# A two-layer graph network: counting edges with one matmul a group, weighing a node's own row by its number of self-edges, and spreading one step of the sort over five groups

## The chip, the core and the metric

The kernel runs on one core of a Trainium2 chip. The metric is the time of one whole execution on the device, in microseconds (us); before the change it is 2135.78 us, the median of three runs from 2135.06 to 2137.22. The five engines named below run their own instruction streams in the order in which the program gave them: TensorE (PE) for matmuls and transposes, VectorE (DVE), ScalarE (ACT), GpSimd (POOL), which here issues the indirect DMAs, and SyncE (SP), which here issues the plain ones.

## The reference

There are 6250 nodes of 512 float32 values and 106,250 directed edges: 50,000 random ones, the same ones reversed, and one self-edge for each node, all sorted by destination. Among the random ones a few are self-edges too, so a node can have more than one. Two layers follow each other:

```python
# layer 0 (edges sorted by dst)
agg = segment_sum((x @ W_l.T + b_l)[src], dst);  deg = segment_sum(1, dst)
x   = layernorm(x + agg / max(deg, 1) + x @ W_r.T)
# layer 1 (sums over src: the edges have to be sorted by src)
neigh = segment_sum((x[dst] @ W_neigh.T + b_neigh), src) / max(segment_sum(1, src), 1)
h   = x + relu(x @ W_self.T + b_self + neigh)
h   = layernorm(h) * gamma + beta
x   = layernorm(x + h)
```

The text calls them first and second layer. Both take a mean over a node's edges of rows gathered from a table (the input x, then the first layer's result h), and multiply mean and own row by one 512x512 matrix each.

## The kernel before

**Tiles, windows, groups.** The sorted edges lie 128 to a tile, one edge on each partition. POOL gathers the 128 rows of a tile with one indirect DMA from the table (`gather`, L603, issued at L604): 128 rows of 2 KB. The nodes are cut into windows of at most 32 consecutive ones, and four windows (C = 4) far apart in the list make a group, which fills 128 partitions. The first layer has 831 tiles, 238 windows and 60 groups; the second 782 tiles, 261 windows and 66 groups, since the sort of the second layer drops each node's first self-edge, whose row is the node's own and needs no gathering. The groups at the end have three windows. A buffer named `rows` holds one tile for each of the four windows, and there are ten such buffers (CHUNKS), so gathers can run ahead of their use by up to ten of them.

**One group.** `fetch` (L608) issues the group's gathers, about 14 in the first layer and 12 in the second (nine in the last three groups). `match` (L628) makes the 0/1 matrix `hot` on DVE: for every tile and window, which of the window's 32 nodes the edge on each partition belongs to. `visits` (L685) sums the rows: one matmul per tile and window, `hot` (128x32) against the gathered rows (128x512), into `agg` in PSUM (L694). `shrink` (L636) makes a bfloat16 copy `hotb` of `hot` on ACT (L639). `count` (L697) multiplies `hotb`, tile by tile, by a column of ones, which gives the number of edges of each node in `deg` (L703): 600 such matmuls in all, four or five a group. `inverse` (L553) makes one over it on DVE (L557 in the second layer, L560 to L563 in the first). `average` (L708) multiplies `agg` by it on ACT (L714). `turn` transposes on PE (L569), `dense` multiplies by the two weight matrices (L577), `close` and `store` (L732) do the rest of the layer on DVE and write the group's rows through SP (L743), or, for three groups of each layer, through POOL with an indirect scatter (L736). `begin` (L669) loads the group's own rows through SP (L682).

**Self-edges in the second layer.** The first self-edge of each node is added as the node's own row: `average` adds `own` to `agg` on DVE before the mean (L712, shown under the line of the helper `both`, L173), and `inverse` adds 1 to the count (L557). Self-edges beyond the first, of which up to 64 are allowed (CAP), are put into one extra tile of rows, `more_rows`, gathered once at the head of the second layer (L611, by the list `more_i`). Every group of the second layer visits it like a tile of its own (X = 1), at the head of `visit_tiles`: 522 matmuls in all, eight instructions a group with their weight loads.

**What packs that list.** The second layer's sort runs inside the first layer's groups. `sort_and_place` (L891) yields it as small pieces, and `more` takes one PE piece and up to five DVE pieces out of the list at the end of each group. The last two PE pieces are `loops_beyond_one` (L386) and `place` (L441). `loops_beyond_one` finds the self-edges beyond the first among the last 51 columns of sorted edges, numbers them, builds one 0/1 matrix for each column on DVE (in chunks of 14 columns, in one buffer `hots`), and multiplies it with the column on PE (L430) into 64 slots; 102 matmul instructions. It is one piece. `place` then finds where the windows begin.

**The order of the work.** There is no planner: on each engine the instructions stand in the program's order. The loop at the end of `grouped` writes that order out by hand. In one turn of it, gathers and `hot` of group g+1 come first, then visits of group g in three parts, with the transposes and matrix products of group g-1 between them, then count and average of g, the finish of g-1, a piece of the sort, and `hotb` of g+1.

Of the kernel before, what the change touches and what calls it, by code (L numbers as in the profile page):

```python
# [19 lines left out]
C = 4  # L20
# [78 lines left out]
def kernel(  # L99
# [109 lines left out]
    class Sorter:  # L209


        def __init__(self, key, val, layer, pool, ps, loops):


            self.pool, self.ps, self.layer, self.loops = pool, ps, layer, loops
            self.M = M if not loops else (E - N + P - 1) // P
            pair = self.pair = PAIR_L if loops else PAIR
            self.half = (pair + 1) // 2
            self.vis = self.half + 1
            self.NW = (2 * self.M + pair - 1) // pair  # L220
# [12 lines left out]
            self.flag = const.tile([1, 1], I32, name=f"flag{layer}")  # L233
            if loops:

                a = (E - N - CAP - 1) // P
                self.row = pool.tile([P, M - a], F32, name="row")
                nc.gpsimd.iota(self.row, pattern=[[P, M - a]], base=a * P - (E - N) + LOOP,
                               channel_multiplier=1, allow_small_or_imprecise_dtypes=True)
                self.more = const.tile([P, 1], F32, name="more")  # L240
                self.more_i = const.tile([P, 1], I32, name="more_i")
# [144 lines left out]
        def loops_beyond_one(self):  # L386
# [35 lines left out]
            per = W // CAP  # L422
            hots = self.fresh()
            for m in range(0, n, per):
                k = min(per, n - m)
                hot = hots[:, :k * CAP].rearrange("p (k c) -> p k c", c=CAP)
                both(hot, number[:, m:m + k].unsqueeze(2).to_broadcast([P, k, CAP]),
                     iota[:, :CAP].unsqueeze(1).to_broadcast([P, k, CAP]), ALU.is_equal)
                for i in range(k):
                    nc.tensor.matmul(p[:CAP, D + 2:D + 3], hot[:, i, :], node[:, m + i:m + i + 1],  # L430
                                     start=m + i == 0, stop=m + i == n - 1)
# [6 lines left out]
            nc.vector.tensor_scalar(none, self.more, float(N - 1), None, op0=ALU.min)  # L438
            nc.vector.tensor_copy(self.more_i, none)
# [113 lines left out]
    def inverse(deg, nr, work, loops=False):  # L553

        inv = work.tile([P, 1], F32, name="inv")
        if loops:
            nc.vector.tensor_scalar(inv[:nr], deg, 1.0, None, op0=ALU.add)  # L557
            nc.vector.reciprocal(inv[:nr], inv[:nr])
            return inv, None
# [20 lines left out]
    def grouped(s, table, w_n, w_s, layer, finish, dest, other):  # L580


        with tc.tile_pool(name=f"g{layer}", bufs=2) as work, tc.tile_pool(
# [24 lines left out]
            def fetch(g):  # L608
                if g == 0 and s.loops:
                    rows = work.tile([P, D], F32, name="more_rows", bufs=1)  # L610
                    nc.gpsimd.indirect_dma_start(  # L611
                        out=rows, out_offset=None, in_=table,
                        in_offset=bass.IndirectOffsetOnAxis(ap=s.more_i[:, :1], axis=0))
                    chunks["more"] = {c: rows for c in range(C)}
# [21 lines left out]
            def shrink(g):  # L636
                hb = work.tile([P, (s.X + s.vis) * C, H], BF16, name="hotb", bufs=1)
                n = len(visit_tiles(g)) * C
                nc.scalar.copy(hb[:, :n], hots[g][:, :n])  # L639
# [45 lines left out]
            def visits(g, some):  # L685
# [4 lines left out]
                for v, t in list(enumerate(visit_tiles(g)))[some]:  # L690
                    for c in windows(g):
                        ts = [u for u in visit_tiles(g) if c in chunks[u]]
                        if t in ts:
                            nc.tensor.matmul(agg[H * c:H * (c + 1), :], hot[:, C * v + c, :],  # L694
                                             chunks[t][c], start=t == ts[0], stop=t == ts[-1])

            def count(g):  # L697
                st, hb = state[g], hots[g][1]
                nr = st["nr"]
                deg = ps.tile([P, 1], F32, name="deg")  # L700
                n = len(visit_tiles(g))
                for v in range(n):
                    nc.tensor.matmul(deg[:nr],  # L703
                                     hb[:, C * v:C * v + nr // H, :].rearrange("p c h -> p (c h)"),
                                     ones_b, start=(v == 0), stop=(v == n - 1))
# [55 lines left out]
            for g in range(Q + 1):  # L761
# [5 lines left out]
                if g < Q:  # L767
                    visits(g, slice(0, 2 + s.X))
# [172 lines left out]
```

## Time and profile before

| | |
|---|---|
| time, three runs | 2135.78 us (2135.06 to 2137.22) |
| the profiled execution's own time | 2607.48 us |
| its span, first to last instruction | 2605.5 us |
| mean granted TensorE clock | 0.904 of full speed |
| PE busy | 1986.7 us, 76%, 8653 matmul instructions |
| POOL busy | 1554.8 us, 60% |
| DVE busy | 1045.7 us, 40% |
| ACT busy | 368.7 us, 14% |
| visits, L694 (gathered tiles; `more_rows`) | 4220 instructions, 780.1 us; 522, 71.4 us |
| count, L703 | 600 instructions, 35.8 us, 167 ns each |
| `hotb`, L639 | 126 casts, 86.3 us, 685 ns each |
| `agg` plus `own`, L173 | 66, 46.2 us, 700 ns each |
| packing's matmuls, L430 | 102 instructions, 11.4 us |
| `more_rows` gather, L611 | 1, 1.0 us |

Durations and waits come from one profiled execution, which here took 2607.48 us where the timed runs took 2135.78. A profile line names the source line, the engine, the operation, what it writes and reads, how often it ran, its busy time and the mean of one in ns, and the idle time of the engine just before it with what ended it. "Issue" stands for idle time for which the profile shows no cause. A row of a timeline has the start in us from the span's first instruction, the duration, then engine, line and operation; a bracket at its end holds the engine's idle time ahead of it and what ended that. Several equal instructions that follow each other are one row (x4).

### The profile page before, as it was taken

Reading aid. Unit: us, or ns where it says so; the run is one execution under the profiler, and the core shown is the slowest. Engines: PE = TensorE matmul, PEld = TensorE weight load, DVE = VectorE, ACT = ScalarE, POOL = GpSimd, SP = SyncE. Lnnn points to the kernel's source line nnn. Section 1 sums busy time; section 2 is a strip of 40 time slices with the busy share of each in tenths; the row PEclk is TensorE's granted clock in tenths of the full one; section 3 lists DMA queues with packets and bytes.
Section 4 is the critical chain, followed back from the end, with each engine's and each line's share of the span. In section 5 each row is a group of like instructions: output and inputs, shape, how many; then the busy total and the mean of one; then the engine's idle time right before and its main releaser. Section 6 shows DMA issues by size and latency. Waiting matters only on the chain.

```text
span 2605.5 us, 27728 instructions
## 1 busy us (share of the span) xinstructions
PE 1986.7 (76%) x8653; PEld 725.9 (28%) x8653; DVE 1045.7 (40%) x2301; ACT 368.7 (14%) x721; POOL 1554.8 (60%) x1639
## 2 busy tenths in 40 slices
PE   4186876877778676776674888888888888888896
PEld 1022322322322223322220232332323223232332
DVE  2244333344444343211220454444544445454465
ACT  0011111111111111111110111111111111111121
POOL 4566666666666664566526666666656666666641
PEclk9698888888898887898886999999999999999999
DMA  7666766666676664666526676666666676666752
GB/s 222 182 196 203 211 198 204 207 202 202 201 209 202 204 201 147 179 205 205 164 79 183 201 203 202 204 206 204 198 200 204 201 210 199 202 194 204 206 170 59
DMA packets 184614, 499.74 MB, mean 192 GB/s; under 512 B 43962, under 2 KB 46452, under 8 KB 184446
## 3 DMA queue, kind: packets, MB, share of 16 engines
q0 software_dynamic: 130208, 426.37, 56.3%
q1 hardware_dynamic: 51406, 65.89, 8.0%
q10 hardware_dynamic: 2832, 5.51, 0.6%
q8 instruction: 74, 1.21, 0.2%
q14 instruction: 94, 0.77, 0.1%
HBM read 465.01 MB, written 32.96 MB: 191 GB/s over the span
## 4 chain that ended last, share of the span: by engine, by line
PE 37%; issue 14%; another core or an unknown queue 12%; DVE 9%; SPq 4%; ACT 1%; DMA 1%; POOL 0%; DVEq 0%; POOLq 0%; ACTq 0%
PE po L577 19%; PE agg L694 14%; PE tp L569 3%; SPq L743 2%; SPq L644 1%; SPq L682 1%; DVE stats L505 1%; DVE agg L173 1%; DVE po L173 1%; DVE srt L173 1%; ACT mean L714 1%; DVE hot L173 1%; DVE po L515 1%; DVE y L515 1%
## 5 line engine op out<-in xcount | busy, mean ns | idle before, releaser
L604 POOL DMA_INDIRECT rows<-in_x_dram,idx x834 | 799.9, 959 | 468.4 <-issue 238.8
L604 POOL DMA_INDIRECT rows<-h_d,idx x785 | 744.6, 948 | 437.1 <-issue 211.3
L694 PE MATMUL agg<-rows,hot 128*32 128x512 f32 x4220 | 780.1, 633 | 222.9 <-issue 186.0
L577 PE MATMUL po<-wa,meanT 128*128 128x512 f32 (+1 forms) x1008 | 492.2, 633 | 86.8 <-issue 81.3
L577 PE MATMUL po<-wb,ownT 128*128 128x512 f32 (+1 forms) x1008 | 488.6, 630 | 0.3
L694 PEld LDWEIGHTS agg<-rows,hot 128*32 128x32 f32 x4220 | 148.4, 111 | 657.9 <-issue 589.7
L560 DVE TENSOR_SCALAR inv<-deg 128x1 f32<-128x1 f32 (+1 forms) x60 | 9.5, 158 | 786.2 <-remote 312.5
L577 PEld LDWEIGHTS po<-wa,meanT 128*128 128x128 f32 (+1 forms) x1008 | 189.8, 198 | 391.1 <-issue 382.1
L569 PE MATMUL tp<-ident,mean 128*128 128x128 f32 (+1 forms) x504 | 97.5, 325 | 215.0 <-ACT mean L714 146.0
L557 DVE TENSOR_SCALAR inv<-deg 128x1 f32<-128x1 f32 (+1 forms) x66 | 10.5, 158 | 619.6 <-remote 401.4
L577 PEld LDWEIGHTS po<-wb,ownT 128*128 128x128 f32 (+1 forms) x1008 | 196.1, 206 | 207.3 <-issue 204.5
L571 ACT COPY ownT<-tp 128x512 f32<-128x512 f32 (+1 forms) x126 | 73.3, 582 | 1193.2 <-remote 495.9
L173 DVE SCALAR_TENSOR_TENSOR srt<-srt 128x448 f32<-128x448 f32 (+3 forms) x313 | 180.7, 618 | 4.6
L569 PEld LDWEIGHTS tp<-ident,mean 128*128 128x128 f32 (+1 forms) x504 | 63.1, 162 | 350.0 <-ACT mean L714 218.3
L714 ACT ACTIVATE mean<-agg,inv 128x512 f32<-128x512 f32 (+1 forms) x126 | 86.6, 687 | 391.1 <-DVE some L563 83.1
L509 ACT ACTIVATE rstd<-mv,eps 128x1 f32<-128x1 f32 (+1 forms) x192 | 56.6, 295 | 426.1 <-DVE mv L507 204.0
L571 ACT COPY meanT<-tp 128x512 f32<-128x512 f32 (+1 forms) x126 | 72.5, 575 | 183.6 <-remote 122.2
L173 DVE SCALAR_TENSOR_TENSOR hot<-rel,cols 128x640 f32<-128x640 f32 x126 | 96.2, 765 | 0.1
L639 ACT CAST hotb<-hot 128x640 bf16<-128x640 f32 x126 | 86.3, 685 | 24.5 <-DVE hot L173 24.5
L569 PEld LDWEIGHTS tp<-ident,own 128*128 128x128 f32 (+1 forms) x504 | 62.6, 141 | 67.5 <-issue 65.5
L694 PE MATMUL agg<-more_rows,hot 128*32 128x512 f32 x522 | 71.4, 611 | 13.1 <-DMA rows<-h_d,idx 13.1
L569 PE MATMUL tp<-ident,own 128*128 128x128 f32 (+1 forms) x504 | 75.2, 272 | 0.0
(154 smaller groups left out, 968.1 us busy)
## 6 DMA issues: line engine op xcount, KB each, us to landing
own<-h_d SPq DMA_DIRECT2D x261, 64.0 KB
out_dram<-y SPq DMA_DIRECT2D x250, 64.0 KB
own<-in_x_dram SPq DMA_DIRECT2D x230, 64.0 KB
h_d<-y SPq DMA_DIRECT2D x227, 64.0 KB
rows<-in_x_dram,idx POOLq DMA_INDIRECT x834
rows<-h_d,idx POOLq DMA_INDIRECT x785
wa<-in_L_gnn_W_l_dram ACTq DMA_DIRECT2D x1, 1024.0 KB
wb<-in_L_gnn_W_r_dram ACTq DMA_DIRECT2D x1, 1024.0 KB
```

The costliest lines, as they stand in the source:

```text
L173: nc.vector.scalar_tensor_tensor(o, a, 1.0, b, op0=ALU.mult, op1=op)
L505: nc.vector.bn_stats(stats[:nr], v)
L509: nc.scalar.activation(root[:nr], mv[:nr, 1:2], AF.Sqrt, bias=eps[:nr])
L515: nc.vector.tensor_scalar(y, v, mv[:nr, 0:1], root[:nr], op0=ALU.subtract, op1=ALU.mult)
L569: nc.tensor.transpose(p[:, k, :nr], v[:nr, k * P:(k + 1) * P], ident[:nr, :nr])
L571: nc.scalar.copy(t[:, :, :nr], p[:, :, :nr])
L577: nc.tensor.matmul(po[:nr], aT[:, k, :nr], w[:, k, :], start=first and k == 0, stop=end and k == NK - 1)
L604: nc.gpsimd.indirect_dma_start(out=t, out_offset=None, in_=table, in_offset=bass.IndirectOffsetOnAxis(ap=s.idx[:, m:m + 1], axis=0))
L639: nc.scalar.copy(hb[:, :n], hots[g][:, :n])
L694: nc.tensor.matmul(agg[H * c:H * (c + 1), :], hot[:, C * v + c, :], chunks[t][c], start=t == ts[0], stop=t == ts[-1])
L714: nc.scalar.mul(st["mean"][:nr], st["agg"][:nr], st["inv"][:nr])
L743: put.append(nc.sync.dma_start(dest[ds(start(c * Q + g, dest), H), :], y[H * c:H * (c + 1)]))
```

## The change

- **Count.** `shrink` no longer casts `hot`. It sums `hot` over the tiles of the group on DVE (`tensor_reduce`, with a stride, since the tiles are the outer index) and writes the sum, 128x128 in bfloat16, into `hotb`. `count` is then one matmul, into a column of `deg`. In the second layer ACT copies the part of `hot` that marks the extra self-edges into a second half of `hotb`, and a second matmul counts them by themselves.
- **Own row.** `average` in the second layer adds `own` times (1 + number of extra self-edges) to `agg`, in one instruction on DVE, instead of `own` once. The count's inverse takes one more small DVE operation.
- **No extra tile of rows.** `more_rows`, its gather, its list `more_i` and its visits are gone; the parts of the visits are cut at the same gathered tiles as before (0:2, 2:3, 3:).
- **Packing in pieces.** `loops_beyond_one` is now a generator with five pieces; each of the later ones has the matmuls of up to 14 columns, whose matrices were made in the piece before, in two halves of `hots` with seven columns each. It takes five groups, and `place` comes four groups later.

```diff
-                self.more_i = const.tile([P, 1], I32, name="more_i")
+                self.parts = 2 + (M - a - 1) // (W // CAP // 2 * 2)
...
-            per = W // CAP
+            per = W // CAP // 2
             hots = self.fresh()
-            for m in range(0, n, per):
+
+            def hot(m):
                 k = min(per, n - m)
-                hot = hots[:, :k * CAP].rearrange("p (k c) -> p k c", c=CAP)
-                both(hot, number[:, m:m + k].unsqueeze(2).to_broadcast([P, k, CAP]),
+                v = hots[:, m // per % 2 * per * CAP:][:, :k * CAP].rearrange(
+                    "p (k c) -> p k c", c=CAP)
+                both(v, number[:, m:m + k].unsqueeze(2).to_broadcast([P, k, CAP]),
                      iota[:, :CAP].unsqueeze(1).to_broadcast([P, k, CAP]), ALU.is_equal)
-                for i in range(k):
-                    nc.tensor.matmul(p[:CAP, D + 2:D + 3], hot[:, i, :], node[:, m + i:m + i + 1],
-                                     start=m + i == 0, stop=m + i == n - 1)
+                return v
+
+            ready = [(m, hot(m)) for m in range(0, min(2 * per, n), per)]
+            while ready:
+                yield
+                for m, v in ready:
+                    for i in range(v.shape[1]):
+                        nc.tensor.matmul(p[:CAP, D + 2:D + 3], v[:, i, :],
+                                         node[:, m + i:m + i + 1],
+                                         start=m + i == 0, stop=m + i == n - 1)
+                m += per
+                ready = [(m, hot(m)) for m in range(m, min(m + 2 * per, n), per)]
...
-    def inverse(deg, nr, work, loops=False):
+    def inverse(deg, nr, work):
         inv = work.tile([P, 1], F32, name="inv")
-        if loops:
-            nc.vector.tensor_scalar(inv[:nr], deg, 1.0, None, op0=ALU.add)
-            nc.vector.reciprocal(inv[:nr], inv[:nr])
-            return inv, None
...
             def fetch(g):
-                if g == 0 and s.loops:
-                    rows = work.tile([P, D], F32, name="more_rows", bufs=1)
-                    nc.gpsimd.indirect_dma_start(
-                        out=rows, out_offset=None, in_=table,
-                        in_offset=bass.IndirectOffsetOnAxis(ap=s.more_i[:, :1], axis=0))
-                    chunks["more"] = {c: rows for c in range(C)}
...
             def visit_tiles(g):
                 t = own_tiles(g)
-                return ["more"] * s.X + list(range(t.start - 1, t.stop))
+                return range(t.start - 1, t.stop)
...
             def shrink(g):
-                hb = work.tile([P, (s.X + s.vis) * C, H], BF16, name="hotb", bufs=1)
-                n = len(visit_tiles(g)) * C
-                nc.scalar.copy(hb[:, :n], hots[g][:, :n])
+                hb = work.tile([P, 1 + s.X, C * H], BF16, name="hotb", bufs=1)
+                n = s.X + len(visit_tiles(g))
+                with nc.allow_low_precision("whole numbers up to 5"):
+                    nc.vector.tensor_reduce(
+                        hb[:, 0, :], hots[g][:, s.X * C:n * C].rearrange(
+                            "p (v c) h -> p (c h) v", c=C),
+                        axis=mybir.AxisListType.X, op=ALU.add)
+                if s.X:
+                    nc.scalar.copy(hb[:, 1, :], hots[g][:, :C].rearrange("p c h -> p (c h)"))
                 hots[g] = (hots[g], hb)
...
             def count(g):
-                deg = ps.tile([P, 1], F32, name="deg")
-                n = len(visit_tiles(g))
-                for v in range(n):
-                    nc.tensor.matmul(deg[:nr],
-                                     hb[:, C * v:C * v + nr // H, :].rearrange("p c h -> p (c h)"),
-                                     ones_b, start=(v == 0), stop=(v == n - 1))
-                st["inv"], st["some"] = inverse(deg[:nr], nr, work, s.loops)
+                deg = ps.tile([P, 2], F32, name="deg")
+                for i in range(1 + s.X):
+                    nc.tensor.matmul(deg[:nr, i:i + 1], hb[:, i, :nr], ones_b,
+                                     start=True, stop=True)
+                if not s.loops:
+                    st["inv"], st["some"] = inverse(deg[:nr, :1], nr, work)
+                    return
+                st["some"] = None
+                for n in ("loops", "inv"):
+                    st[n] = work.tile([P, 1], F32, name=n)
+                nc.vector.tensor_scalar(st["loops"][:nr], deg[:nr, 1:2], 1.0, None, op0=ALU.add)
+                nc.vector.tensor_tensor(st["inv"][:nr], deg[:nr, :1], st["loops"][:nr],
+                                        op=ALU.add)
+                nc.vector.reciprocal(st["inv"][:nr], st["inv"][:nr])
...
                 if s.loops:
-                    both(st["agg"][:nr], st["agg"][:nr], st["own"][:nr], ALU.add)
+                    nc.vector.scalar_tensor_tensor(st["agg"][:nr], st["own"][:nr],
+                                                   st["loops"][:nr], st["agg"][:nr],
+                                                   op0=ALU.mult, op1=ALU.add)
...
-                    visits(g, slice(0, 2 + s.X))
+                    visits(g, slice(0, 2))
...
-                    visits(g, slice(2 + s.X, 3 + s.X))
+                    visits(g, slice(2, 3))
...
-                    visits(g, slice(3 + s.X, None))
+                    visits(g, slice(3, None))
...
-        yield True, s.loops_beyond_one
+        parts = s.loops_beyond_one()
+        for _ in range(s.parts):
+            yield True, lambda: next(parts, None)
         yield True, s.place
```

More of the change, by code (lines that the diff above doesn't have):

```diff
@@ L437, in loops_beyond_one @@
             nc.vector.tensor_scalar(self.more, self.more, float(-LOOP), None, op0=ALU.add)
-            nc.vector.tensor_scalar(none, self.more, float(N - 1), None, op0=ALU.min)
-            nc.vector.tensor_copy(self.more_i, none)
         def place(self):
@@ L625, in visit_tiles @@
                 t = own_tiles(g)
-                return ["more"] * s.X + list(range(t.start - 1, t.stop))
+                return range(t.start - 1, t.stop)
             def match(g):
                 hot = work.tile([P, (s.X + s.vis) * C, H], F32, name="hot")
-                n = len(visit_tiles(g)) * C
+                n = (s.X + len(visit_tiles(g))) * C
                 both(hot[:, :n], s.rel[:, g].rearrange("p v c -> p (v c)")[:, :n].unsqueeze(2)
@@ L636, in shrink @@
             def shrink(g):
-                hb = work.tile([P, (s.X + s.vis) * C, H], BF16, name="hotb", bufs=1)
-                n = len(visit_tiles(g)) * C
-                nc.scalar.copy(hb[:, :n], hots[g][:, :n])
+                hb = work.tile([P, 1 + s.X, C * H], BF16, name="hotb", bufs=1)
[7 more added lines that the diff above has]
+                    nc.scalar.copy(hb[:, 1, :], hots[g][:, :C].rearrange("p c h -> p (c h)"))
                 hots[g] = (hots[g], hb)
@@ L693, in visits @@
                         if t in ts:
-                            nc.tensor.matmul(agg[H * c:H * (c + 1), :], hot[:, C * v + c, :],
+                            nc.tensor.matmul(agg[H * c:H * (c + 1), :],
+                                             hot[:, C * (s.X + v) + c, :],
                                              chunks[t][c], start=t == ts[0], stop=t == ts[-1])
```

## The prediction

> **What bounds the kernel now.** I read the groups first, then the timelines of the layers' ends and middle, and put the result beside the times. The groups (columns: executions, busy us, mean ns of one, idle us before them):
>
> ```profile
> L604 POOL DMA_INDIRECT rows<-in_x_dram,idx x834 | 799.9, 959 | 468.4 <-issue 238.8
> L604 POOL DMA_INDIRECT rows<-h_d,idx x785 | 744.6, 948 | 437.1 <-issue 211.3
> ...
> L639 ACT CAST hotb<-hot 128x640 bf16<-128x640 f32 x126 | 86.3, 685 | 24.5 <-DVE hot L173 24.5
> ...
> L694 PE MATMUL agg<-more_rows,hot 128*32 128x512 f32 x522 | 71.4, 611 | 13.1 <-DMA rows<-h_d,idx 13.1
> ```
>
> PE is busiest by its share (76% against POOL's 60%), so one would take PE for the bound. The timeline of the second layer's start says otherwise:
>
> ```profile
> 1370.91 0.95 POOL L604 DMA_INDIRECT rows<-h_d,idx  x1 [0.30 <-issue]
> 1372.17 0.95 POOL L604 DMA_INDIRECT rows<-h_d,idx  x1 [0.30 <-issue]
> 1373.42 0.95 POOL L604 DMA_INDIRECT rows<-h_d,idx  x1 [0.30 <-issue]
> 1376.91 0.28 PE L703 MATMUL deg<-ones_b,hotb 128*128 128x1 bf16 x5
> ```
>
> A POOL that waits for nothing starts a gather every 1.25 us: 0.95 of work and a gap of 0.30 that follows every gather. Group 0's last gather starts at 1372.17 and its count at 1376.91: PE is 4.7 us behind, so transfers keep up. In the middle of the layer it looks different:
>
> ```profile
> 2219.23 1.03 PE L694 MATMUL agg<-rows,hot 128*32 128x512 f32 x4
> 2222.40 1.02 PE L694 MATMUL agg<-rows,hot 128*32 128x512 f32 x2 [2.14 <-issue]
> 2225.72 0.94 POOL L604 DMA_INDIRECT rows<-h_d,idx  x1 [4.28 <-PE agg L694]
> ```
>
> PE sits between its instructions with "issue" named, on rows gathered some 50 us before, and POOL waits for it. These waits are in the profiled execution (2607.48 us) and, I infer, hardly in the timed runs (2135.78 us). The proof is a sum of POOL's schedule with those waits left out, from rows alone:
> - first gather at 30.4;
> - layer 1: 834 x (0.959 + 0.305) = 1054.2, two other gathers and two iotas 3.0;
> - handover: 4.7 to the last group's count, 0.7 by which PE's last group (12.0) exceeds its nine gathers (11.3), 19.4 from that count (1333.9) to the next gather (1353.3): 24.8;
> - layer 2: the extra gather 1.3, 785 x (0.948 + 0.305) = 983.6, two scatters in the queue 2.6;
> - end: 4.7, PE's lag in the last three groups 2.2 (below), and 23.8 from the last count (2581.7) to 2605.5: 30.7.
>
> Sum 2130.6; with the 2.0 around the span 2132.6, against 2135.8 timed: 0.15% short. So in the timed runs **POOL's gather rate sets the time**, 12 gathers = 15.0 us a group in layer 2, about 14 = 17.6 in layer 1, while PE without those waits needs 14.2 (2523.34 to 2537.55) in layer 2 and 14.0 (991.93 to 1005.93) in layer 1.
>
> **The change, part by part.** Lines are those of before.
>
> *The extra gather* (L611): one POOL gather at the head of layer 2, 1.00 + 0.30: **-1.3 us**. The other gathers, the own loads and the stores keep number and order in the POOL and SP queues.
>
> *The extra visits* (L694, more_rows): 522 instructions, eight a group, pitch about 0.88 us a group, so 58 us of PE. In steady state this lies inside POOL's 15.0 us and is worth nothing. It counts where PE is behind POOL: the last three groups have three windows, nine gathers (11.3 us), and PE takes 12.9:
>
> ```profile
> 2537.55 0.28 PE L703 MATMUL deg<-ones_b,hotb 128*128 128x1 bf16 x5
> 2537.76 1.06 PE L694 MATMUL agg<-more_rows,hot 128*32 128x512 f32 x6
> 2539.03 0.69 ACT L714 ACTIVATE mean<-agg,inv 128x512 f32<-128x512 f32 x1 [1.78 <-DVE agg L173]
> 2540.47 0.66 PE L569 MATMUL tp<-ident,mean 128*128 128x128 f32 x4
> 2550.43 0.38 PE L703 MATMUL deg<-ones_b,hotb 128*96 128x1 bf16 x5
> ```
>
> The lag is 3 x (12.9 - 11.3) less two scatters on POOL (2.6) = 2.2. Without the extra visits the transposes could start at 2539.6, but the mean ends at 2539.72, plus one more small DVE operation (0.18) and less 0.09 for a shorter count: about 2540.0. So 0.5 of the 0.88 is gained: 12.4 a group, lag 0.7, gain 1.5. Against it the reduction (below) stands in DVE's queue; in the iteration that also computes the last group's slots DVE then has 13.3, which gives back up to 0.9. I take **-1.0** (bounds 0 and -2.5).
>
> *Count products* (L703): 600 become 192; at 0.03 apart, 0.1 us a group, hidden by POOL's 15.0. On the path only at the two layer ends: **-0.2** in all.
>
> *Average* (L712): same operation, 0.70, with a scalar; one more DVE operation of 0.16-0.18 before it (row L557, 0.158). Hidden but at the last group: **+0.2**. Behind it wait ACT's mean and PE's transposes, which lag POOL by nothing.
>
> *The cast becomes a reduction* (L639): 126 ACT casts of 0.685 go (66 small copies of about 0.3 come); 126 DVE reductions over 512 or 640 elements come. Nearest rows: BN_STATS over 512, 0.695; TENSOR_REDUCE over 896, 1.086; so 0.70 and 0.83. These read contiguously and the new one with a stride: bounds 0.7 and, by guess, three times that. DVE is busy 48.3 of 100 us at 18 us a group, 8.7 a group, in layer 2 and about as much in layer 1; 9.6 fits under 15.0. It delays match(g+2) and store(g-1), which PE and SP need a group later: **0**. Uncovered it would cost 126 x 0.75 = 95 us. [...] The rows: gathers take 959 ns beside the sort's two-input operations (layer 1) and 948 in layer 2, where BN_STATS with one input stands beside them: 834 x 0.011 = 9 us, so contention exists and is small. [...] I take 0.
>
> *Packing in five pieces* (L386). Before, it is one block (PE, DVE, POOL of one timeline):
>
> ```profile
> 1005.93 0.28 PE L703 MATMUL deg<-ones_b,hotb 128*128 128x1 bf16 x5
> 1019.73 0.16 DVE L560 TENSOR_SCALAR inv<-deg 128x1 f32<-128x1 f32 x1 [18.35 <-remote]
> 1022.70 0.67 PE L401 MATMUL turn<-node,srt 128*128 128x51 f32 x2 [16.48 <-DVE srt L395]
> 1040.68 3.64 PE L694 MATMUL agg<-rows,hot 128*32 128x512 f32 x16
> 1042.91 0.97 POOL L604 DMA_INDIRECT rows<-in_x_dram,idx  x1 [23.33 <-PE agg L694]
> ```
>
> PE does no visit for 34 us, 21 of them real work (1019.7 to 1040.7), and POOL stalls 23.3, since in this execution it was already ten tiles ahead. In the timed runs POOL is about 5 us ahead; ten tiles of four gathers, one in use, leave 36 gathers = 45 us before POOL must wait. 34 < 45, so the block is hidden now and splitting it gains **0** (bounds 0 and -23.3). PE catches up afterwards, 17.6 against 14.0 a group. `place` moves four groups back, to about 49 of 60: ten groups of cover; if that were gone, 10 us of DVE work.
>
> [...] The windows show granted clocks of 0.95-0.98 in layer 2 and 0.83-0.95 in layer 1, where PE waits more. If layer 2 fell to 0.87, its group would take about 13.4/0.87 = 15.4, 0.4 over POOL's pace: up to 25 us over 66 groups if lasting. [...] I take 0.
>
> Sum: -1.3 - 1.0 - 0.2 + 0.2 = -2.3: **2133.5 us**. (0.2%, 4.3 us, is about what a measurement of this kernel can tell from no change.)
>
> **Rivals.**
> 1. *The packing stall is real in the timed runs*: POOL does wait as in the trace. Against it: the sum above leaves 3 us for such stalls. For it: the sum's terms could be off by 10. Gain 10 to 23 more: 2111-2124.
> 2. *PE sets the pace in the timed runs too*: layer 2 gains 0.5 to 1.0 a group (33 to 64), counts in layer 1 6, packing 23: about -78, 2058. For: PE 76% busy, POOL waiting for it 277 us. Against: the sum.
> 3. *Slower: the strided reduction blocks POOL's descriptor work.* Place: 126 reductions, each beside a gather three times in four (0.95 of 1.25). Price in full 126 x 0.75 x 0.75 = 71 us: 2205; it decides from 0.05 us a reduction (6.6 us against the gain of 2.3). Against: BN_STATS rows. For: no strided reduction stands in the trace.
>
> **How the numbers follow.** POOL as the bound 0.70, its own range 2129-2137 (tail and handover terms, run spread 2 us), of which 0.28 lies over 0.2% faster and 0.03 slower; rival 1 0.12, rival 2 0.08, rival 3 (clock loss with it) 0.10. Faster 0.20 + 0.12 + 0.08 = 0.40; slower 0.02 + 0.10 = 0.12; same 0.48. The range reaches down through rival 1 and leaves out rivals 2 and 3: 2112 to 2138.
>
> **What would show it.** Gathers of 0.95 + 0.30 as before; a reduction near 0.75; POOL idle before L604 may shrink a lot in the profile, since the stalls sit in PE's dense runs of small instructions, of which 930 go: the profiled time may fall far more than the timed one. The 23.3 us stall gone. Wrong if the timed gain exceeds 10 us (PE or packing was on the path), or if gathers lengthen beside the reduction.

## The result

The changed kernel takes 2131.47 us (median of 10 runs, 2129.01 to 2134.15), the kernel before beside it 2136.5 (10 runs, 2134.4 to 2138.93). The ratio is 0.9979, 95% interval 0.9971 to 0.9988: 4.5 us, with 2.6 to 6.2 in the interval. Forecast were 2133.5 us and a gain of 2.3.

One fact has to be known before any number below is read: the kernel before takes 2136 us on some chips and 2568 to 2570 on others, each time in all runs of a series. E1 to E4 ran on one chip of the second kind and E5 to E8 on another; E9 and E10 ran on one of the first kind, E11 and E12 on another. I call them the 2568 chips and the 2136 chips. Each chip ran one series, so that it is the chip, and not something else that lasts through a series, is inferred. The result and the profile after have the times of a 2136 chip, and the profile ahead of the prediction (2607.48) looks like those of a 2568 chip. Every ratio is against the kernel before in the same series.

### The profile page after: what moved, and what is told of

Read it like the earlier page. It is cut to its first block, busy times and chain, and to the rows that moved or that the text cites. A ratio compares the mean times of both kernels' runs of the same rounds, so it can differ in the third digit from the quotient of the medians.

```text
span 2129.2 us, 26081 instructions
## 1 busy us (share of the span) xinstructions
PE 1945.1 (91%) x7723; PEld 671.4 (32%) x7723; DVE 1185.0 (56%) x2495; ACT 314.6 (15%) x661; POOL 1554.9 (73%) x1638
## 4 chain that ended last, share of the span: by engine, by line
DMA 32%; POOL 28%; PE 22%; issue 14%; DVE 3%; POOLq 0%; ACT 0%; SPq 0%; DVEq 0%; ACTq 0%
POOL rows L609 28%; DMA rows<-h_d,idx 17%; DMA rows<-in_x_dram,idx 14%; PE po L582 10%; PE agg L700 9%; PE tp L574 2%; DMA val_i<-in_dst_dram 0%; DVE stats L514 0%; PE turn L465 0%; DVE po L173 0%; DMA own<-in_x_dram,slots 0%; PE deg L709 0%; PE turn L438 0%; PE turn L294 0%; DVE agg L727 0%
## 5 line engine op out<-in xcount | busy, mean ns | idle before, releaser
L700 PE MATMUL agg<-rows,hot 128*32 128x512 f32 x4220 | 900.3, 612 | 134.0 <-DMA rows<-in_x_dram,idx 46.1
L609 POOL DMA_INDIRECT rows<-in_x_dram,idx x834 | 800.7, 960 | 266.4 <-issue 224.7
L582 PE MATMUL po<-wa,meanT 128*128 128x512 f32 (+1 forms) x1008 | 466.0, 605 | 0.0
L582 PE MATMUL po<-wb,ownT 128*128 128x512 f32 (+1 forms) x1008 | 456.3, 596 | 0.1
L565 DVE TENSOR_SCALAR inv<-deg 128x1 f32<-128x1 f32 (+1 forms) x60 | 9.5, 158 | 490.4 <-PE deg L709 490.4
L582 PEld LDWEIGHTS po<-wb,ownT 128*128 128x128 f32 (+1 forms) x1008 | 181.8, 190 | 183.6 <-issue 183.4
L718 DVE TENSOR_SCALAR loops<-deg 128x1 f32<-128x1 f32 (+1 forms) x66 | 10.4, 158 | 310.9 <-PE deg L709 302.4
L640 DVE TENSOR_REDUCE hotb<-hot 128x128 bf16<-128x512 f32 (+1 forms) x126 | 133.8, 1062 | 0.1
L574 PEld LDWEIGHTS tp<-ident,mean 128*128 128x128 f32 (+1 forms) x504 | 52.8, 141 | 110.7 <-issue 43.5
L574 PE MATMUL tp<-ident,mean 128*128 128x128 f32 (+1 forms) x504 | 82.8, 287 | 4.8 <-ACT mean L731 4.8
L524 DVE TENSOR_SCALAR po<-po,mv,rstd 128x512 f32<-128x512 f32 (+1 forms) x66 | 54.0, 818 | 2.4
```

Of the source, the lines that this page charges most:

```text
L524: nc.vector.tensor_scalar(y, v, mv[:nr, 0:1], root[:nr], op0=ALU.subtract, op1=ALU.mult)
L565: nc.vector.tensor_scalar(inv[:nr], deg, 1.0, None, op0=ALU.max)
L574: nc.tensor.transpose(p[:, k, :nr], v[:nr, k * P:(k + 1) * P], ident[:nr, :nr])
L582: nc.tensor.matmul(po[:nr], aT[:, k, :nr], w[:, k, :], start=first and k == 0, stop=end and k == NK - 1)
L609: nc.gpsimd.indirect_dma_start(out=t, out_offset=None, in_=table, in_offset=bass.IndirectOffsetOnAxis(ap=s.idx[:, m:m + 1], axis=0))
L640: nc.vector.tensor_reduce(hb[:, 0, :], hots[g][:, s.X * C:n * C].rearrange("p (v c) h -> p (c h) v", c=C), axis=mybir.AxisListType.X, op=A ...
```

## The profile after

The groups of the changed kernel (executions, busy us, mean ns of one, idle us before them and what ended it), to be held against those of before:

```profile
L700 PE MATMUL agg<-rows,hot 128*32 128x512 f32 x4220 | 900.3, 612 | 134.0 <-DMA rows<-in_x_dram,idx 46.1 <-DMA rows<-h_d,idx 42.4 <-DVE hot L173 28.6
L609 POOL DMA_INDIRECT rows<-in_x_dram,idx x834 | 800.7, 960 | 266.4 <-issue 224.7 <-DMA rows<-in_x_dram,idx 25.6 <-PE agg L700 8.2
L609 POOL DMA_INDIRECT rows<-h_d,idx x785 | 744.9, 949 | 242.6 <-issue 200.3 <-DMA rows<-h_d,idx 17.1 <-PE tp L574 11.6
L640 DVE TENSOR_REDUCE hotb<-hot 128x128 bf16<-128x512 f32 (+1 forms) x126 | 133.8, 1062 | 0.1
L709 PE MATMUL deg<-ones_b,hotb 128*128 128x1 bf16 (+1 forms) x192 | 24.2, 174 | 0.0
```

The gathers take what they took, 960 and 949 ns. POOL's idle time before them is 266 us for 834 gathers and 243 for 785, which is 0.32 and 0.31 each: hardly more than the gap of 0.30 that follows every gather, where the profile of before had 468 and 437. What PE's visits wait for is now the landing of rows. The reduction is 1.06 us on average, against my 0.70 to 0.83. The timeline in the middle of the second layer shows the same at close range:

```profile
2050.08 0.95 POOL L609 DMA_INDIRECT rows<-h_d,idx  x1 [0.30 <-issue]
2051.33 0.94 POOL L609 DMA_INDIRECT rows<-h_d,idx  x1 [0.30 <-issue]
2052.05 0.20 PE L709 MATMUL deg<-ones_b,hotb 128*128 128x1 bf16 x2
2054.69 1.04 PE L700 MATMUL agg<-rows,hot 128*32 128x512 f32 x2 [0.60 <-DMA rows<-h_d,idx]
2056.16 1.05 PE L700 MATMUL agg<-rows,hot 128*32 128x512 f32 x2 [0.43 <-DMA rows<-h_d,idx]
```

A gather every 1.25 us, and PE behind it, waiting for each tile. The span is 2129.2 at a mean granted clock of 0.984. It would be wrong to read 2605.5 minus 2129.2 as the change's work: the two profiles are, as far as I can infer, from chips of different kinds.

## Experiments on the 2568 chips: the parts, and what holds PE there

**E1. The kernel before, unchanged.**

> The kernel before, unchanged: a second profiled execution, and the noise of a comparison. Theory A (POOL's gathers set the time of the timed runs; the long waits of the first profile belong to that execution): the span comes out at 2132 to 2137 us, L604 at 1.25 us from gather to gather in the middle of both layers, POOL's waits for PE gone but for the packing and the layers' ends; ratio 1.000. Theory B (PE is the bound and the profile shows the kernel as it is): the profile shows again more than 60 waits of about 4 us in each layer, and a span near 2600.

Measured: 2568.45 us against 2567.83, ratio 0.9999 (0.9989 to 1.001); span 2569.0. On this chip the waits are no matter of one profiled execution: the runs have the same time as the profile. Its waits of POOL (us in total, times, longest) and, from the start of the second layer, rows of PE's and DVE's timeline, then the busy time of the engines in a stretch of it:

```profile
POOL rows L604 <- issue: 444.9, 1394, 12.7
POOL rows L604 <- PE agg L694: 263.8, 78, 25.9
```

```profile
1361.87 0.28 PE L703 MATMUL deg<-ones_b,hotb 128*128 128x1 bf16 x5
...
1377.02 1.01 PE L694 MATMUL agg<-rows,hot 128*32 128x512 f32 x1 [1.79 <-issue]
1379.82 1.01 PE L694 MATMUL agg<-rows,hot 128*32 128x512 f32 x1 [1.79 <-issue]
1382.62 1.01 PE L694 MATMUL agg<-rows,hot 128*32 128x512 f32 x1 [1.79 <-issue]
...
1409.94 0.16 DVE L557 TENSOR_SCALAR inv<-deg 128x1 f32<-128x1 f32 x1 [71.04 <-remote]
```

```profile
core 0: us, PE busy (x) PEld busy (x) DVE busy (x) ACT busy (x) POOL busy (x), PEclk, DMA share, GB/s
1365.00:1400.00 35.00, 11.30 (x12) 1.35 (x11) 0.00 (x0) 0.59 (x1) 26.47 (x29) 0.55 0.72 210
```

In these 35 us POOL issues 29 gathers without a pause and PE gets one matmul done every 2.80 us, with nothing that the profile can name between them. DVE does nothing at all, and not for want of data: its next operation, the inverse of group 0's count, starts at 1409.94, though PE ended that count at 1362.15. The stall ends some 7 us after POOL has filled its ten buffers and stopped (1403.1). From then on a shorter stall comes in nearly every group, in which POOL waits about 3 us.

**E2 to E4. One part of the change each, on the kernel before.** E2, the packing alone:

```diff
-        yield True, s.loops_beyond_one
+        parts = s.loops_beyond_one()
+        for _ in range(s.parts):
+            yield True, lambda: next(parts, None)
```

> The packing in five pieces alone; extra tile, casts and count products as before. Theory A (the block of 34 us lies behind the 45 us that POOL may run ahead): 0 us, ratio 0.999 to 1.001. Rival 1 (the packing stall is on the path in timed runs): -3 us or more, so that most of the 5 us that the whole change gained is here, ratio below 0.9985.

Measured: 2553.99 us, ratio 0.9956 (0.9942 to 0.997), by the ratio 11.3 us. E3, the extra tile alone; `hotb` stays a cast and the count stays a product for each tile:

```diff
-                return ["more"] * s.X + list(range(t.start - 1, t.stop))
+                return range(t.start - 1, t.stop)
...
+                nc.tensor.matmul(deg[:nr, 1:2],
+                                 hb[:, :nr // H, :].rearrange("p c h -> p (c h)"),
+                                 ones_b, start=True, stop=True)
...
-                    both(st["agg"][:nr], st["agg"][:nr], st["own"][:nr], ALU.add)
+                    nc.vector.scalar_tensor_tensor(st["agg"][:nr], st["own"][:nr],
+                                                   st["loops"][:nr], st["agg"][:nr],
+                                                   op0=ALU.mult, op1=ALU.add)
```

> The extra tile alone taken out: no gather of it, no visits to it, own row weighed by 1 + the number of extra self-edges, counted by a product of its own beside the four or five for the gathered tiles; casts on ACT and packing in one block as before. Theory A: -1.3 for the gather, -0.5 to -2.5 at the layer's end, +0.2 for the longer chain: -2 us, ratio 0.9985 to 0.9995. If PE is on the path in layer 2: -30 us or more.

Measured: 2551.29 us, ratio 0.9935 (0.992 to 0.995), by the ratio 16.7 us. E4, the count alone; the extra tile stays, so the sum takes its part of `hot` in:

```diff
-                nc.scalar.copy(hb[:, :n], hots[g][:, :n])
+                nc.vector.tensor_reduce(
+                    hb, hots[g][:, :n * C].rearrange("p (v c) h -> p (c h) v", c=C),
+                    axis=mybir.AxisListType.X, op=ALU.add)
...
-                for v in range(n):
-                    nc.tensor.matmul(deg[:nr],
-                                     hb[:, C * v:C * v + nr // H, :].rearrange("p c h -> p (c h)"),
-                                     ones_b, start=(v == 0), stop=(v == n - 1))
+                nc.tensor.matmul(deg[:nr], hb[:, :nr], ones_b, start=True, stop=True)
```

> The count alone changed: the sum over tiles on DVE instead of the cast on ACT, one product a group; extra tile and packing as before. Theory A: DVE's 126 reductions of about 1.06 us lie under POOL's pace: 0 us, between -1 and +1, ratio 0.9995 to 1.0005. Rival 3 (the reduction holds up POOL): slower, +3 us or more.

Measured: 2543.48 us, ratio 0.9909 (0.9895 to 0.9922), by the ratio 23.4 us. All three lie far outside what I expected of a kernel at POOL's pace. E3 and E4 take instructions off PE, which is stalled here; E2 only moves some. Each is worth several times what it is on a 2136 chip (E9 to E11), and why so much isn't shown. They say nothing about how the gain of the result is made up.

**E5. The whole change there.**

> The changed kernel unchanged, beside the kernel before on the same chip. Where the kernel before takes 2136 us, 0.998 again. Where it takes 2568 us, the three parts measured there should add: 0.0044 + 0.0065 + 0.0091 = 0.020, ratio 0.980, 2516 us; if they save the same stall, less: 0.991.

Measured: 2532.66 against 2570.02, ratio 0.9858 (0.9829 to 0.9887), by the ratio 36.5 us. The parts sum to 0.020 and the whole is 0.0142, as if they saved partly the same stall; that isn't shown, since the parts ran on another chip of this kind. So the change is worth 0.2% on one kind of chip and 1.4% on the other.

**E6 and E7. Another order on PE.** In the traces that I had looked at, stalls started 30 to 33 matmuls after the last dense product (counted over the whole traces it is less sharp: those over 1 us at the visits start mostly after 29 to 36 in E1, and anywhere from 6 to 35 in E5). I took that for a supply of instructions running dry in a long run of short matmuls, and broke the run up; nothing else is changed, E6 on the changed kernel and E7 on the one before:

```diff
-                    visits(g, slice(0, 2))
+                    visits(g, slice(0, 1))
                 if g:
-                    turn(g - 1, "mean")
                     dense(g - 1, "own")
+                if g < Q:
+                    visits(g, slice(1, 2))
+                if g:
+                    turn(g - 1, "mean")
```

> The changed kernel with another order on PE, nothing else: half of the first visits, then the own rows' dense product, then the other half, then the mean's transposes; before, all first visits and the transposes stood in one run. The same instructions on every engine. Theory F (where the kernel before takes 2568 us, PE's supply of instructions runs dry when more than about 31 short matmuls follow each other, since in each of the traces the stall starts 30 to 33 matmuls after the last dense product): the longest run is now about 22, so the stalls of 4 us a group go and the time falls to about 2130, POOL's pace, ratio 0.83. Theory G (these waits are for rows, for the mean or for semaphores, or belong to the chip's clock): the order changes little, within 20 us of the changed kernel, ratio 0.975 to 0.99. Where the kernel before takes 2136: POOL's pace by both, 0.995 to 1.003.

> The kernel before with the same order on PE, and nothing of the change (in the second layer the run in the middle has the extra tile's visits with it, 28 matmuls). Theory F: about 2135 where the kernel before takes 2568, ratio 0.83 to 0.85. Theory G: ratio 0.99 to 1.00. Where it takes 2136: 1.000 within 0.003.

Measured: E6 2577.74 us, ratio 1.0036 (1.0015 to 1.0056), 45 us slower than the changed kernel; E7 2638.65, ratio 1.0258 (1.0185 to 1.0331). Theory F falls: the stalls did not go with the long runs. Theory G had the order change little, which isn't so either. PE's matmul waits in E6 show a new one, at the head of the list:

```profile
PE po L582 <- DVE v L173: 173.4, 32, 14.1
PE po L582 <- issue: 139.9, 49, 7.5
PE tp L574 <- issue: 97.1, 19, 16.2
```

The dense product moved up now waits for DVE to have read the former group's `po`, 32 times for 173 us. The waits on "issue" stay beside it: those of visits, transposes and dense products together are about 257 us in E6 and 265 in E5.

**E8. One more gather in each group.** The changed kernel gathers one tile more in every group, into a buffer that nothing reads:

```diff
+                    if t == own_tiles(g).start:
+                        gather(work.tile([P, D], F32, name="spare", bufs=1), g)
```

> The changed kernel with one more gather in each of the 126 groups, of a tile that nothing reads. If POOL's gathers set the time: 126 x 1.25 = +158 us, ratio 1.072 where the kernel before takes 2136. If PE does (where it takes 2568): hidden in POOL's waits of about 4 us a group, 0 to +20 us over the changed kernel, ratio 0.98 to 0.99.

Measured: 2700.44 us, ratio 1.0518 (1.0485 to 1.0552). Against E5 that is 167.8 us for 126 gathers, 1.33 each, a little more than the 1.25 that POOL needs. So even on a 2568 chip gathers aren't hidden under PE's stalls, and PE isn't the bound in the plain sense: a group there takes POOL's gathers and a stall on top, that does not shrink when POOL has more to do. POOL's waits before `rows` that end with PE's visits or on "remote" (a releaser that the profile can't name) are 363 us in E5 and 365 in E8. That PE is held up while gathers stream, and let go after POOL has stopped, is what the rows of E1 show; what holds it is open (at the end).

## Experiments on the 2136 chips: where the 5 us are

**E9. The packing in one block again**, the rest as changed (the diff of E2 backwards, with its chunks of 14 columns).

> The changed kernel with the packing put back into one block, all else as changed. Where the kernel before takes 2136 us: my prediction's step (the block is covered by POOL's lead of 45 us) says that nothing is lost, ratio to before 0.9975 to 0.9982, as the changed kernel; rival 1 (the block's stall is on the path) says that most of the 5 us goes, 0.999 to 1.000, and the profile shows POOL waiting 3 us or more at one place near 900. Where the kernel before takes 2568: 0.9858 was the whole change and 0.0044 the pieces alone, so 0.990 if they add.

Measured: 2130.4 us, ratio 0.9972 (0.9961 to 0.9982). Nothing is lost. The timeline of E9 around the block, with PE's and POOL's rows:

```profile
838.87 0.18 PE L697 MATMUL deg<-ones_b,hotb 128*128 128x1 bf16 x1
842.06 0.67 PE L400 MATMUL turn<-node,srt 128*128 128x51 f32 x2 [3.01 <-DVE srt L394]
...
854.28 1.53 POOL L597 DMA_INDIRECT rows<-in_x_dram,idx  x1 [0.30 <-issue]
855.04 5.07 PE L429 MATMUL turn<-node,srt 128*64 128x1 f32 x46 [1.18 <-DVE srt L173]
...
860.04 3.64 PE L688 MATMUL agg<-rows,hot 128*32 128x512 f32 x16
860.29 0.95 POOL L597 DMA_INDIRECT rows<-in_x_dram,idx  x1 [0.30 <-issue]
```

PE does no visit from 838.9 to 860.0, 21 us, and POOL never stops: its gap stays 0.30. Three gathers beside the block's wide DVE operations are longer (1.33, 1.53 and 1.38 where 0.95 is usual). The block is covered, as forecast, and cutting it up gains nothing here.

**E10. Each reduction twice.**

```diff
+                    nc.vector.tensor_reduce(
+                        hb[:, 0, :], hots[g][:, s.X * C:n * C].rearrange(
+                            "p (v c) h -> p (c h) v", c=C),
+                        axis=mybir.AxisListType.X, op=ALU.add)
```

> The changed kernel with each of the 126 reductions made twice, 134 us more on DVE. Where the kernel before takes 2136: covered by POOL's 15.0 us a group, +0 to +2 us over the changed kernel (the layer's last group), ratio 0.998 to 0.999; if DVE were on the path or blocked POOL, up to +134, 1.06. Where it takes 2568: within 10 us of the changed kernel there, 0.984 to 0.990.

Measured: 2130.37 us, ratio 0.9971 (0.9959 to 0.9983), the same as the changed kernel. The groups of E10, whose columns are those of the first fence:

```profile
L609 POOL DMA_INDIRECT rows<-in_x_dram,idx x834 | 801.6, 961 | 266.5 <-issue 228.4 <-DMA rows<-in_x_dram,idx 21.6 <-PE agg L704 6.7
L609 POOL DMA_INDIRECT rows<-h_d,idx x785 | 743.4, 947 | 242.3 <-issue 199.8 <-DMA rows<-h_d,idx 16.1 <-PE tp L574 11.6
L644 DVE TENSOR_REDUCE hotb<-hot 128x128 bf16<-128x512 f32 (+1 forms) x126 | 137.9, 1094 | 4.3
```

138 us more on DVE, and the gathers are 961 and 947 ns where they were 960 and 949. The strided reduction neither fills DVE's group nor slows POOL: rival 3 is out. In E10's trace the last count ends 10.3 us after the last gather, against 9.0 in the changed kernel's: at the layer's end, as the expectation allowed, a doubled reduction may show.

**E11. The extra tile put back.** The changed kernel with its gather, its visits and the plain addition of `own` (E4's edits with the packing in pieces).

> The changed kernel with the extra tile put back: its gather at the head of the second layer, eight visits a group, own row added once; the count by the reduction and one product, the packing in pieces. Where the kernel before takes 2136 us: if the extra tile is what was worth 5 us, 0.9995 to 1.0005, and the profile's handover is 1.3 us longer and its end 2 to 4 us longer than the changed kernel's; if the casts and the count products were, 0.997 to 0.998. My sum had 2.1 of 2.3 us for the extra tile: 0.9985 to 0.999. Where it takes 2568: 0.9858 / 0.9935 = 0.992.

Measured: 2133.69 us (13 runs), ratio 0.9991 (0.9983 to 1.0). It lies between the two kernels: 2.2 to 3.3 us above the changed kernel, E9 and E10 (2131.47, 2130.4 and 2130.37), and 2.7 below the kernel before (2136.35). By these medians about half of the gain is the extra tile's, near what I had for it. The other half would have come with the count (the packing is worth nothing by E9), to which I had given 0.2; its size is loose: 2.7 us by the medians, 1.9 by the ratio, and the interval of E11 reaches from 0 to 3.6 us.

**E12. The kernel before, for a profile on a 2136 chip.**

> The kernel before, unchanged, for a profile on this chip beside the others of this call. Where it takes 2136 us: the same sum by POOL's rows as in the prediction, 1.25 us a gather without long waits, span 2132 to 2137; the terms by which it exceeds the changed kernel's 2129.2 (head 30.4, first layer's gathers 1056.3, handover 24.5, second layer's gathers 984.2, end 33.8) tell where the 5 us lay: handover and end by the extra tile, the middle of the layers by anything else.

Measured: 2136.68 us against 2136.35, ratio 1.0001 (0.9992 to 1.001); span 2135.3. Its waits of POOL, in the columns of E1:

```profile
POOL rows L604 <- issue: 430.2, 1371, 12.8
POOL rows L604 <- PE agg L694: 11.6, 38, 0.3
POOL more_rows L611 <- DVE hot L173: 3.5, 1, 3.5
```

POOL's waits for PE's visits are 38, none over 0.3 us, which is its gap (the longest wait on "issue", 12.8, is the one before the first gather). Where the prediction had to leave the waits out by arithmetic, this trace has none to leave out. The span, cut at POOL's first and last gather of each layer, beside E11 and the changed kernel:

| us | before (E12) | tile back (E11) | changed |
|---|---|---|---|
| to the first gather | 30.5 | 30.7 | 30.4 |
| first layer, first to last gather | 1058.5 | 1056.0 | 1056.3 |
| handover, to the second layer's first gather of `rows` | 27.3 | 25.6 | 24.5 |
| second layer, first to last gather | 985.0 | 984.0 | 984.2 |
| from the last gather to the end | 33.9 | 33.6 | 33.8 |
| span | 2135.3 | 2129.9 | 2129.2 |

Each column is one execution, and of E11 a short one (2131.81 us, where its median is 2133.69); differences under 1 us are within what such columns vary by.

## Why the prediction held, and where its sum was off

**The bound: right, and for the right reason.** POOL's sum of 2130.6 stands against a span of 2135.3 in E12, 4.7 short, which is twice the gain that I forecast; so it tells the bound, not the gain. The terms: gathers of the first layer 1057.2 with the four small operations (1058.5 measured), handover 24.8 and 1.3 (27.3), second layer 983.6 (985.0), end 30.7 and 2.6 for two scatters in the queue (33.9), first gather 30.4 (30.5). No term is off by more than 1.5. Rival 2 is out on the 2136 chips, since POOL waits over its gap for PE's visits in neither trace.

**What I said of the waits: wrong.** I put the waits of 4 us a group down to the one profiled execution. E1 has them on its chip, where all runs take the time of the profile. The arithmetic held because the runs were timed on a chip without them, and that was luck: where E5 was timed, the changed kernel takes 2532.66, and the forecast of 2133.5 would have missed by 400 us and the change's gain by 34.

**The extra gather: right.** Handover of the kernel before (E12), then of the changed one:

```profile
1098.04 5.37 PE L577 MATMUL po<-wb,ownT 128*96 128x512 f32 x8
1110.67 0.93 POOL L736 DMA_INDIRECT h_d<-y,slots  x1 [14.58 <-DVE y L515]
1115.06 1.00 POOL L611 DMA_INDIRECT more_rows<-h_d,more_i  x1 [3.46 <-DVE hot L173]
1116.37 0.97 POOL L604 DMA_INDIRECT rows<-h_d,idx  x1 [0.30 <-issue]
```

```profile
1095.69 3.67 PE L582 MATMUL po<-wb,ownT 128*96 128x512 f32 x8
1106.62 0.93 POOL L753 DMA_INDIRECT h_d<-y,slots  x1 [13.82 <-DVE y L524]
1111.16 1.00 POOL L609 DMA_INDIRECT rows<-h_d,idx  x1 [3.61 <-DVE hot L173]
```

From 1115.06 to 1116.37 are the 1.3 us. The rest of the difference in the handover, 1.5, stands in the first line of each: the same eight matmuls take 5.37 in one and 3.67 in the other. That is the clock, by the busy time of the engines in these stretches (granted clock behind POOL's busy time), of E12 and then of the changed kernel:

```profile
1098.00:1104.00 6.00, 5.96 (x10) 2.18 (x11) 1.57 (x4) 0.66 (x2) 0.00 (x0) 0.72 0.16 37
```

```profile
1095.00:1100.00 5.00, 4.86 (x14) 2.08 (x15) 2.20 (x5) 0.66 (x2) 0.00 (x0) 1.00 0.07 16
```

In E11 the clock is 1.00 there too, with the tile in place, so the tile alone doesn't bring it; E9 and E10 have 3.67 for these matmuls as well. Whether the kernel before has the low clock at this place always or in this execution alone, one trace can't say.

**The extra visits: the step was right, a second one ate it.** I had the lag of the last groups fall from 2.2 to 0.7. From the last gather to the last count's end it fell from 10.4 (E12) to 9.0, by 1.3 against my 1.5. But from there to the end it grew from 23.6 to 24.8, where I had 0.2. E11 first, then the changed kernel, from the last count on:

```profile
2106.22 0.20 PE L717 MATMUL deg<-ones_b,hotb 128*96 128x1 bf16 x1
2108.31 0.55 PE L581 MATMUL tp<-ident,mean 96*128 96x96 f32 x4 [1.89 <-ACT mean L726]
2108.70 3.60 PE L589 MATMUL po<-wb,ownT 128*96 128x512 f32 x8
```

```profile
2104.19 0.25 PE L709 MATMUL deg<-ones_b,hotb 128*96 128x1 bf16 x2
2106.55 0.90 PE L574 MATMUL tp<-ident,mean 96*128 96x96 f32 x4 [2.12 <-ACT mean L731]
2107.25 4.97 PE L582 MATMUL po<-wb,ownT 128*96 128x512 f32 x8
```

Eight matmuls at 4.97 instead of 3.60: a granted clock of 0.50 for a part of them (2106.59 to 2110.00 below), in the last group of the path, 1.4 us. The changed kernel, E9 and E10 all have it there (4.97, 5.29 and 5.28), E11 and E12 don't (3.60 in both). So the step that failed is the one on the clock, where I took 0, which no run had shown. I asked only whether a low clock would last through the layer, which it doesn't (0.984 over the span), and never asked it of the one group that has nothing beside it. There the clock of 0.50 follows 2.12 us of idle PE.

What decides may be when the idle time falls: in each of the five traces with 2136-chip times, the stretches of half clock (0.50) all begin on one grid of 3.41 us; the changed kernel's has nine, each beginning a whole number of 3.413 us after the first, and so do the 60 of the profile ahead of the prediction. Two windows of that grid from the changed kernel, before and after its clock falls, then the two that hold E11's idle time:

```profile
2103.17:2106.59 3.42, 1.30 (x11) 0.36 (x9) 2.01 (x6) 1.16 (x2) 0.00 (x0) 1.00 0.17 41
2106.59:2110.00 3.41, 3.41 (x8) 1.70 (x9) 2.91 (x6) 0.66 (x2) 0.00 (x0) 0.50 0.00 0
```

```profile
2103.73:2107.15 3.42, 2.69 (x14) 0.88 (x12) 0.65 (x3) 0.48 (x1) 0.00 (x0) 1.00 0.24 60
2107.15:2110.56 3.41, 2.25 (x9) 1.19 (x10) 2.91 (x7) 1.34 (x3) 0.00 (x0) 1.00 0.00 0
```

In the changed kernel, E9 and E10 the 2.12 us lie whole in one window, where PE is busy for 1.3 us; in E11 and E12 the grid cuts the idle time in two, and PE is busy for 2.25 us or more in each window. So it may be chance, from one execution to the next, whether the last group pays the 1.4 us; five traces don't settle that. Nor does the busy time in a window settle it: at the handover PE is busy for 2.09 us of the window before and idle for 1.22 in one piece in E12, where half the clock follows (0.72 on average from 1098 to 1104), and for 2.08 and 1.24 in the changed kernel, where it doesn't (1.00 from 1095 to 1100). What decides stays open.

**Average: right.** Count to mean is 1.51 in E12 (2111.35 to 2112.86) and 1.63 changed (2104.19 to 2105.82): 0.12 against my 0.2.

**Count and reduction: probably mis-sized.** I had 0 for the reduction and 0.2 for the products; E11 gives 2.7 by the medians and 1.9 by the ratio, with 0 to 3.6 in its interval. The reduction itself takes 1.06 us where I had 0.70 to 0.83. My 0 held in one sense: DVE covers it, and twice of it (E10). That the gathers would pay nothing for it was an assumption too, since no row of before has a strided reduction; with one in each group they take 960 and 949 ns on average, with two 961 and 947 (E10). What is left is not a wait: POOL's idle time before the first layer's gathers is the same in E12, E11 and the changed kernel (266.6, 266.5 and 266.4 us). In these traces it would be the handover's clock (1.7) and the gathers' own length in the first layer, 802.8 us in E12 against 800.3 in E11, 800.7, 801.3 and 801.6 in the changed kernel, E9 and E10. With one profile of the kernel before I don't call either shown.

**Packing: right.** 0 on a 2136 chip (E9), with the cover that the step named. Rival 1 is out.

So the forecast of 2.3 was half of the measured 4.5 to 5.0, by the count's term, which E11 puts at 1.9 to 2.7 and I had at 0.2, and with two clock effects of 1.4 and 1.7 us, one against and one perhaps for the change, that the sum didn't have. A gain of 0.21% lies on the border of 0.2% that I had drawn between "same" (0.48) and "faster" (0.40), and the range of 2112 to 2138 was wide beside it: the experiments test the parts, the total hardly does.

## What to carry to other kernels

When the timed runs are much shorter than the profiled execution, sum the bound engine's schedule from its rows without waits and hold it against the timed runs; if it closes within half a percent, as here, that speaks for that engine as the one that sets the time, and a trace without the waits (E12) settles it. Work taken from any other engine is then worth only what it moves at the ends of the stages: here 138 us more on DVE left the time where it was (E10, 2130.37 us against 2131.47). At those ends, where one chain runs alone, ask for the clock of every short wait: 2.1 us of idle PE went with eight matmuls at 4.97 instead of 3.60 us, and 1.2 us went with a low clock in one trace and a full one in four. And if profile and times differ by a fifth, don't call it the profiler: the same program may run so on another chip: this change was worth 0.2% on one kind and 1.4% on the other.

## What the runs showed of the hardware that I had not expected

On a 2568 chip, while POOL streamed gathers without a pause, PE completed one matmul in 2.80 us (E1, 1365 to 1400) with no landing of rows named for the 1.79 us before most of them, ACT and DVE stood almost still (0.59 and 0.00 us busy of 35), and all went on some 7 us after POOL had stopped. In a later stall of the same trace (1707 to 1712) most of SP's instructions start about 0.70 us apart, a quarter of PE's 2.80. On a 2136 chip (E12) the same program does 159 matmul instructions in 35 us of gathers:

```profile
1140.00:1175.00 35.00, 34.32 (x159) 12.07 (x152) 14.25 (x29) 7.24 (x14) 26.58 (x28) 1.00 0.76 224
```

Here POOL is as busy and the DMA rate is higher (224 against 210 GB/s), so neither alone is the cause. I looked for it in runs of short matmuls (E6, E7), and it isn't there; and the clock (0.55 in that stretch of E1) isn't enough: eight matmuls of 512 columns take 3.60 us at the full clock in the rows of the last group above, so at half of it they would take about 7.2, 0.9 each (an estimate), not 2.80. That the engines' supply of instructions is what suffers fits the even steps on several engines, but no run here tells that from other causes. It stays open.
